# A convolution in blocks of four rows by two columns, with its filters transformed over two halves of an attention

## The chip, the cores and the metric

The program runs on one core of one Trainium2 chip. A core has a matrix engine (PE), a vector engine (DVE), an activation engine (ACT), a general engine (POOL) and a queue engine (SP). Each works through its own instructions in order and waits for the others by semaphores. The time is the device time of one launch in microseconds (us); less is better.

## The reference

Two layers, all in float32, on `x` of 4 images, 1024 channels and 32 by 32 pixels:

```python
# layer 0: attention over the 1024 pixels of an image, 16 heads of 64
q, k, v = split(x @ w_qkv.T + b_qkv)          # rotary angles and RMS norm on q and k
ctx = softmax(q @ k.T * scale) @ v
x = x + rmsnorm(ctx @ w_proj.T)
# layer 1: bottleneck, batch norm over images and pixels after each convolution
h = relu(bn(conv1x1(x, w1)))                  # 1024 -> 256 channels
h = relu(bn(conv3x3(h, w2)))                  # 256 -> 256 channels
h = bn(conv1x1(h, w3))                        # 256 -> 1024 channels
return relu(x + softplus(residual_scale) * h)
```

## The kernel before

The batch loop does one image after another: projections of q, k and v (each multiplied as blocks of a fast matrix scheme with few products), then `attention` in two halves of queries (`c` = 0 and 1) of eight head pairs each (`hp`), then the output projection. PE, POOL, DVE and ACT run in the order in which the program is written. That order is made by hand: inside `attention` the lists `late`, `ready`, `slow`, `waiting` and `extra` each give up a step at the end of a head pair, and in the projections `product_done` counts products and releases steps queued by `after`.

For one head pair PE computes the scores `sc` of eight key tiles (L790), ACT takes their exponentials into `p` (L797), DVE adds these into `den` (L814, L816), and PE multiplies `p` by `v` into `cx` (L825). `sc` has three double banks, so PE stands three tiles ahead of ACT at most. Every second head pair a product `dn` (L894) sums the denominators.

`filters` prepares the 3 by 3 filters in the second half of the last image's attention, one step for each of head pairs 1 to 7. Nine taps are loaded into three tiles (L1163); `down_sums` combines three taps in one direction (L1173 to L1176); `fours` and `twos` combine these in the other direction (L1181 to L1188); ACT scales eight results by 1/24 (L1192) and POOL queues them to memory (L1193); `ones_first` and `ones_last` make the other three sets (L1198 to L1204), with six scalings on ACT (L1205 to L1207). The filters `uw` are used in the second convolution.

The output projection follows (L491), and before its second product ACT must copy the last denominators out of a bank (L963). Then the first convolution (L1055, L1014) with partial results `h` and `c` written to memory from a ring of four tiles (`temp`).

The second convolution is done as a Winograd scheme with different block lengths in the two directions: a block of two rows by four columns of outputs comes from a window of four rows by six columns, and each of the 24 positions of the window is one matrix product over the channels. Images go in two pairs (`p`), window positions in three groups of two along the long direction (`g`, with `al` inside) and four along the short one (`j`), output channels in two halves (`f`), input channels in two (`i`). DVE makes the window transforms: `first_cols` (L1524, L1527) and `other_cols` (L1532 to L1537) along the columns, with every fourth pixel read as one operand, and `down` along the rows into the tiles `V` (L1550). `fill` (L1509) applies the norm of the first convolution on ACT. `products` (L1590) makes the products of one key `k` = (p, g, f, al) in a single PSUM bank of eight: first the half with `which` = 0, which ACT copies with swapped sides (`keep`, L1639, L1640), then the other half, which DVE adds (`take`, L1646). `outputs` (L1662 to L1675) makes the four columns from these, again with every fourth pixel written as one operand. `keep`'s copies `m` lie, for the first pair's last group and the whole second pair, in a ring of three (`big_temp`). The statistics of the second norm come from DVE for two images (L1681) and from ACT for two (`act_statistics`, L1689, L1690, whose unused output goes into `temp`). `norm2` (L1697, L1699, L1701) applies the norm. The third convolution (L1829) starts with its first input half and needs `norm2(1)` for the second.

The order in which these steps are issued is a written list at the end; `run` issues products and copies for a stretch of the keys `ks`.

Of the kernel before, what the change touches and what calls it, by code (L numbers as in the profile page):

```python
# [85 lines left out]
def program(ctx, tc, x, wblk, w2, w3, vecs, cos, sin, out, bad):  # L86
# [70 lines left out]
    wd2 = dram.tile([4, len(OUTER), len(SUMS), P, CH], F32, name=f"wd2{u}")  # L157
    u34d = dram.tile([2, 4, P, CH], F32, name=f"u34d{u}")
# [5 lines left out]
    with tc.tile_pool(name=f"st{u}", bufs=2) as st, ExitStack() as s:  # L164
# [987 lines left out]
        uw = {}  # L1152

        def filters():
# [3 lines left out]
            taps = w2.rearrange("p (c k f) -> p c k f", c=NPT, k=9)  # L1158

            def load():  # L1160
                for dx in range(3):
                    for dy, slot in enumerate((0, 1, 3)):
                        nc.gpsimd.dma_start(  # L1163
                            raw[dx][:, slot, :].rearrange("p (c f) -> p c f", c=NPT), taps[:, :, 3 * dy + dx, :]
                        )

# [3 lines left out]
            def down_sums(dx):  # L1170

                g0, g1, new, g2 = (raw[dx][:, i] for i in range(4))
                nc.vector.tensor_tensor(new, g0, g2, ALU.add)  # L1173
                nc.scalar.mul(g1, g1, 0.5)
                nc.vector.scalar_tensor_tensor(g1, new, 0.5, g1, ALU.mult, ALU.add)
                nc.vector.tensor_tensor(new, new, g1, ALU.subtract)  # L1176

            def fours():
                for j in range(4):
                    t = flat(chunk(f"u3_{j}"))  # L1180
                    nc.vector.scalar_tensor_tensor(t, raw[2][:, j], 4.0, raw[0][:, j], ALU.mult, ALU.add)  # L1181
                    plus.append(t)

            def twos():
                for j in range(4):
                    t = flat(chunk(f"u4_{j}"))
                    nc.vector.scalar_tensor_tensor(t, raw[1][:, j], -2.0, plus[j], ALU.mult, ALU.add)
                    nc.vector.scalar_tensor_tensor(plus[j], raw[1][:, j], 2.0, plus[j], ALU.mult, ALU.add)  # L1188
                    minus.append(t)
                for i, ts_ in enumerate((plus, minus)):  # L1190
                    for j, t in enumerate(ts_):
                        nc.scalar.mul(t, t, 1.0 / 24.0)  # L1192
                        nc.gpsimd.dma_start(u34d[i, j], t)  # L1193

            def ones_first():
                for h in range(2):
                    js = slice(2 * h, 2 * h + 2)
                    nc.vector.tensor_tensor(two[h], raw[0][:, js], raw[2][:, js], ALU.add)  # L1198
                    nc.vector.tensor_tensor(raw[1][:, js], two[h], raw[1][:, js], ALU.subtract)

            def ones_last():
                for h in range(2):
                    js = slice(2 * h, 2 * h + 2)
                    nc.vector.scalar_tensor_tensor(two[h], two[h], 2.0, raw[1][:, js], ALU.mult, ALU.subtract)  # L1204
                    nc.scalar.mul(raw[0][:, js], raw[0][:, js], 0.25)  # L1205
                    nc.scalar.mul(raw[1][:, js], raw[1][:, js], -1.0 / 6.0)
                    nc.scalar.mul(two[h], two[h], -1.0 / 6.0)  # L1207

            steps.append(load)
            steps.append(lambda: down_sums(0))  # L1210
            steps.append(lambda: down_sums(2))
            steps.append(lambda: (down_sums(1), fours()))
            steps.append(twos)
            steps.append(ones_first)
            steps.append(ones_last)
# [75 lines left out]
        for b in range(B):  # L1291
# [78 lines left out]
            for c in range(NCH):  # L1370
                if (b, c) == (B - 1, NCH - 1):
                    extra = filters()
# [61 lines left out]
        conv1_first(1, back[1], w)  # L1434
        for i in range(0, NH, 2):
            t_sums(back[1], None, t2[i], i, range(3, 4))
# [20 lines left out]
        if bad is not None:  # L1457
            dt = temp("dens")
            nc.sync.dma_start(dt, dens)
# [22 lines left out]
        TR, TC = H // 2, W // 4  # L1482
# [10 lines left out]
        cols = vp.tile([P, NPT, 6, 2, H + 2, TC], F32, tag="cols", name="cols")  # L1493
        pads = [vp.tile([P, H, W + 4], F32, name=f"pad{i}") for i in range(2)]
        v_tile(0, 0)
        steps_of = vp.tile([P, 4, H, TC], F32, name="steps")
        for i in range(2):
            nc.gpsimd.memset(pads[i], 0.0)
        for i in range(NPT):
            nc.gpsimd.memset(cols[:, i, :, :, :: H + 1, :].rearrange("p a b r c -> p (a b) r c"), 0.0)  # L1500
# [6 lines left out]
        def fill(p, s_, i):  # L1507
            b = PAIRS[p][s_]
            nc.scalar.activation(  # L1509
                pads[s_][:, :, 1 : W + 1], h1[b, i].rearrange("p (a c) -> p a c", a=H), AF.Relu,  # L1510
# [3 lines left out]
        def columns(t):  # L1514
            return t.rearrange("p r (c q) -> p q r c", q=4)

        def first_cols(i, which=range(2)):

            efs = {}
            for s_ in which:  # L1520
                ef = efs[s_] = temp(f"ef_{s_}_{i}").rearrange("p (x r c) -> p x r c", x=2, r=H)
                for x in range(2):
                    d, ahead_ = (columns(pads[s_][:, :, at : at + W])[:, x] for at in (1, 3))
                    nc.vector.scalar_tensor_tensor(ef[:, x], d, -4.0, ahead_, ALU.mult, ALU.add)  # L1524
            for s_ in which:
                for a, op in enumerate((ALU.add, ALU.subtract)):
                    nc.vector.tensor_tensor(cols[:, i, a, s_, 1 : H + 1, :], efs[s_][:, 1], efs[s_][:, 0], op)  # L1527

        def other_cols(s_, i):

            pad, d = pads[s_], steps_of
            nc.vector.tensor_tensor(d, columns(pad[:, :, 2 : W + 2]), columns(pad[:, :, :W]), ALU.subtract)  # L1532
            for a, by in ((2, 2.0), (3, -2.0)):
                nc.vector.scalar_tensor_tensor(
                    cols[:, i, a, s_, 1 : H + 1, :], d[:, 1], by, d[:, 2], ALU.mult, ALU.add
                )
            nc.vector.scalar_tensor_tensor(  # L1537
                cols[:, i, 4:6, s_, 1 : H + 1, :], d[:, 0:2], -4.0, d[:, 2:4], ALU.mult, ALU.add
            )

        def down(p, i, g, js=range(4)):

            c = cols[:, i, 2 * g : 2 * g + 2].rearrange("p a b (r q) c -> p q (a b) r c", q=2)
            d0, d1, d2, d3 = (c[:, k % 2, :, k // 2 : k // 2 + TR] for k in range(4))
            for j in js:
# [3 lines left out]
                out_ = v_tile(p, g)[:, i, j].rearrange("p a b (r c) -> p (a b) r c", r=TR)  # L1549
# [6 lines left out]
        first_cols(0)  # L1556
        down(0, 0, 0, (1, 2))
# [4 lines left out]
        other_cols(0, 0)  # L1562
        conv1(B - 1, 1, 0, w, yt[B - 1])
        other_cols(1, 0)
        down(0, 0, 1, (1, 2))
        conv1(B - 1, 1, 1, w, yt[B - 1], lambda: norm1(1))
        down(0, 0, 0, (0, 3))
        down(0, 0, 1, (0, 3))
        rest()
        open_pools.close()  # L1570
        ps = s.enter_context(tc.tile_pool(name=f"ps2{u}", bufs=8, space=PSUM, reuse_waits="tile"))
# [12 lines left out]
        def products(k, which, i):  # L1584

            p, g, f, al = k
            if k not in banks:
                banks[k] = ps.tile([P, CH], F32, tag="mm", name="c2_" + "_".join(map(str, k)))
            for side, j in enumerate((1, 2) if which == 0 else (0, 3)):
                nc.tensor.matmul(  # L1590
                    banks[k][:, side * QT : (side + 1) * QT],
                    uw[GROUPS[g][al], j][:, i * PL + f * P : i * PL + (f + 1) * P],
                    v_tile(p, g)[:, i, j, al].rearrange("p b t -> p (b t)"),
                    start=which == 0 and i == 0 and side == 0, stop=which == 1 and i == NPT - 1 and side == 1,
                    skip_group_check=True,
                )
# [6 lines left out]
        def x1_home(f):  # L1603

            if f % 3 not in homes:
                tags = (("V1",), ("T0", "T1"), ("T2", "cos", "sin"))[f % 3]
                homes[f % 3] = []
                for tag in tags:
                    pool, rows = (vp, B) if tag == "V1" else (tp, 2 if tag[0] == "T" else 1)
                    t = pool.tile([P, rows, N], F32, tag=tag, name=f"x1_{f}_{tag}")  # L1610
                    homes[f % 3] += [t[:, i] for i in range(rows)]
# [6 lines left out]

        order = {
# [3 lines left out]
        ks = [(p, g, f, al) for p in range(2) for g, f in order[p] for al in range(2)]  # L1623
        flat2 = lambda t: t.rearrange("p b n -> p (b n)")
        mine2 = {f: flat2(h2_all[:, f * B + 2 : f * B + 4, :]) for f in range(NPT)}

        def keep(k):

            p, g, f, al = k
            if p == 0 and g < 2:  # L1630
                m = mine2[f][:, (2 * g + al) * CH : (2 * g + al + 1) * CH]
            else:
                if al == 0:
                    mt[p, g, f] = big_temp(f"m_{p}_{g}_{f}")
                m = mt[p, g, f][:, half[al]]
            mt[k] = m
            rows = m.rearrange("p (r q c) -> p q r c", q=2, c=TC)
            x, y = (banks[k][:, i * QT : (i + 1) * QT].rearrange("p (r c) -> p r c", c=TC) for i in range(2))
            nc.scalar.mul(rows[:, 0], y, -1.0)  # L1639
            nc.scalar.copy(rows[:, 1], x)  # L1640

        def take(p, g, f):
            for al in range(2):
                m = mt[p, g, f, al].rearrange("p (r q c) -> p r q c", q=2, c=TC)
# [285 lines left out]
```

## Time and profile before

| what | us |
|---|---|
| median of three runs | 2693.37 |
| lowest and highest | 2690.72, 2693.93 |
| the profiled execution | 2693.58 |
| its span in the profile | 2691.7 |
| PE busy in it | 2611.6 |
| DVE busy | 2152.3 |
| ACT busy | 1151.5 |
| POOL busy | 462.7 |

Stages of the span, from the timeline and the busy times by stretch:

| stretch (us) | what | PE busy | DVE busy | granted PE clock |
|---|---|---|---|---|
| 0 to 1996 | images 0 to 2, projections of image 3 | 1990.69 | 1609.38 | 1.00 |
| 1996 to 2135 | last attention, first half and a little more | 139.00 | 110.62 | 1.00 |
| 2135 to 2243 | rest of the last attention | 91.40 | 87.99 | 0.94 |
| 2243 to 2328 | last output projection | 84.53 | 70.94 | 0.97 |
| 2328 to 2434 | first convolution | 102.73 | 71.87 | 0.98 |
| 2434 to 2560 | second convolution | 91.09 | 100.02 | 0.89 |
| 2573 to 2692 | third convolution, and the end | 104.28 | 89.07 | 0.94 |

A group line gives the source line, the engine, the operation and the tile names, then the busy time, the mean of one instruction and the idle time ahead of the group with what released it. In a timeline line the first number is the start, the second the length, and the bracket at the end gives the idle time ahead of it. The list of waits adds up idle time by who waited for whom: total, times, longest.

### The profile page before, as it was taken

To read this page: it belongs to the slowest core of one execution; us is meant where nothing else is said; L and a number is where in the kernel's file an instruction comes from. 1 tells how busy PE (TensorE), PEld (TensorE's weight loads), DVE (VectorE), ACT (ScalarE), POOL (GpSimd) and SP (SyncE) were. 2 spreads that over 40 slices of the span, in tenths; PEclk is the share of its full clock that TensorE was granted. 3 is DMA by queue.
4 is the path that set the end of the run, shared out by engine and by line. 5 is a ranking of instruction groups with operands and counts; after the bars stand their busy time and mean duration, and the time that the engine had idled before them with its cause. 6 is when DMAs were issued, how large, how long until landed. Compare 5 with 4: busy or idle time off the path is not lost. (4 is left out here: it accounts for less than half of the span.)

```text
span 2691.7 us, 40390 instructions
## 1 busy us (share of the span) xinstructions
PE 2611.6 (97%) x15308; PEld 1613.5 (60%) x15308; DVE 2152.3 (80%) x2601; ACT 1151.5 (43%) x1678; POOL 462.7 (17%) x610
## 2 busy tenths in 40 slices
PE   9999999999999999999999999999999989998697
PEld 4448433588887333788884335888863326746543
DVE  5668899988888877987978768888887788768787
ACT  2222566533343565233425554333445554212366
POOL 2442323101011222000111221001112320020000
PEclk9999999999999999999999999999999999999899
DMA  7887788667676442665774443666654524671166
GB/s 283 294 243 214 232 260 267 207 202 252 174 196 176 94 86 61 196 197 178 196 203 103 96 81 110 193 223 180 191 142 76 114 89 149 235 231 58 49 224 244
DMA packets 253659, 471.00 MB, mean 175 GB/s; under 512 B 32016, under 2 KB 124992, under 8 KB 253328
## 3 DMA queue, kind: packets, MB, share of 16 engines
q1 hardware_dynamic: 195008, 286.75, 33.6%
q0 software_dynamic: 50384, 164.79, 24.9%
q10 hardware_dynamic: 8064, 16.78, 1.8%
q8 instruction: 124, 2.03, 0.3%
q14 instruction: 79, 0.65, 0.1%
HBM read 331.62 MB, written 99.11 MB: 160 GB/s over the span
## 5 line engine op out<-in xcount | busy, mean ns | idle before, releaser
L797 ACT ACTIVATE p<-sc 128x1024 f32<-128x1024 f32 x512 | 479.9, 1048 | 17.1 <-PE sc L790 16.8
L790 PE MATMUL sc<-q,k 64*64 64x512 f32 x4096 | 456.7, 592 | 11.2 <-ACT p L797 11.2
L825 PE MATMUL cx<-p,to 64*64 64x512 f32 x3072 | 338.2, 589 | 0.0
L790 PEld LDWEIGHTS sc<-q,k 64*64 64x64 f32 x4096 | 150.5, 132 | 305.1 <-ACT p L797 157.3
L816 DVE TENSOR_TENSOR den<-den,p 128x1024 f32<-128x1024 f32 x192 | 237.9, 1239 | 22.9 <-ACT p L797 3.5
L816 DVE TENSOR_TENSOR den_T<-den_T,p 128x1024 f32<-128x1024 f32 x192 | 236.3, 1231 | 20.4 <-DVE den_T L816 1.4
L825 PEld LDWEIGHTS cx<-p,to 64*64 64x64 f32 x3072 | 117.2, 133 | 212.4 <-issue 211.3
L491 PE MATMUL p_y<-q,w_y 128*128 128x256 f32 x928 | 212.6, 382 | 6.7 <-issue 6.7
L486 PE MATMUL p_v<-w_v,x 128*128 128x256 f32 x928 | 210.3, 379 | 2.4 <-DVE x L457 2.3
L491 PEld LDWEIGHTS p_y<-q,w_y 128*128 128x128 f32 x928 | 176.7, 191 | 36.9 <-issue 12.1
L486 PEld LDWEIGHTS p_v<-w_v,x 128*128 128x128 f32 x928 | 176.0, 190 | 28.0 <-DVE x L457 3.3
L831 ACT COPY q<-cx 128x512 f32<-128x512 f32 x64 | 37.5, 585 | 341.3 <-PE cx L825 341.3
L491 PE MATMUL p_q<-to,w_q 128*128 128x256 f32 x672 | 152.2, 379 | 0.0
L491 PE MATMUL p_k<-to,w_k 128*128 128x256 f32 x672 | 152.2, 379 | 0.0
L491 PEld LDWEIGHTS p_q<-to,w_q 128*128 128x128 f32 x672 | 127.4, 190 | 18.4 <-issue 1.2
L491 PEld LDWEIGHTS p_k<-to,w_k 128*128 128x128 f32 x672 | 127.4, 190 | 18.4 <-issue 1.2
L771 POOL TENSOR_SCALAR q<-q,vec 128x512 f32<-128x512 f32 x42 | 81.2, 1943 | 222.1 <-DVE q L770 222.1
L1829 PE MATMUL c<-h,w3t 128*128 128x512 f32 x256 | 111.7, 599 | 5.1 <-ACT h L1699 5.1
L825 PE MATMUL cx<-p,rq 64*64 64x512 f32 x1024 | 112.7, 589 | 0.0
L486 PE MATMUL p_v<-w_v,t 128*128 128x256 f32 x384 | 90.1, 379 | 0.0
L491 PE MATMUL p_y<-to,w_y 128*128 128x256 f32 x384 | 90.1, 379 | 0.0
L1829 PEld LDWEIGHTS c<-h,w3t 128*128 128x128 f32 x256 | 49.2, 192 | 67.1 <-issue 55.7
(545 smaller groups left out, 4334.5 us busy)
## 6 DMA issues: line engine op xcount, KB each, us to landing
w_v<-wd2f SPq DMA_DIRECT2D x112, 256.0 KB
w_y<-wd2f SPq DMA_DIRECT2D x112, 256.0 KB
w_q<-wd2f SPq DMA_DIRECT2D x84, 256.0 KB
w_k<-wd2f SPq DMA_DIRECT2D x84, 256.0 KB
wd2f<-w_pre POOLq DMA_DIRECT2D x68, 256.0 KB, 3.6
q<-qs POOLq DMA_DIRECT2D x64, 256.0 KB, 5.5
k<-ks POOLq DMA_DIRECT2D x64, 256.0 KB, 4.5
x1df<-y POOLq DMA_DIRECT2D x32, 512.0 KB, 5.3
```

Source lines behind the costliest of these rows:

```text
L486: nc.tensor.matmul(o[:, q].rearrange("p (g f) -> p g f", g=2), r[:, i, q * P : (q + 1) * P], wt[:, :, i, :], skip_group_check=True, **at,)
L491: nc.tensor.matmul(o[:, q], wt[:, q, i, :], r[:, i, :], skip_group_check=True, **at)
L771: engine.tensor_scalar(cx, cx, col("bv", hp), None, ALU.add)
L790: nc.tensor.matmul(sc[keys, j], k_all[d, hp, t * P + keys.start : t * P + keys.stop], q_all[d, hp, at], start=True, stop=bad is not None,)
L797: nc.scalar.activation(p, sc, AF.Exp)
L816: nc.vector.tensor_tensor(d_, d_, p, ALU.add)
L825: nc.tensor.matmul(o[j * HD : (j + 1) * HD, i], v[keys, t, h0 : h0 + HD], probs[t][keys, j], start=(t == 0), stop=(t == N // P - 1),)
L831: nc.scalar.copy(cx, o[:, 0])
L1829: nc.tensor.matmul(os[i], w3t[k][f // NH][:, f % NH, :], h2[b, k][:, half[c]], start=(k == 0), stop=(k == NPT - 1),)
```

## The change

The block of the second convolution is turned: four rows by two columns. `first_rows` and `other_rows` now make the sums of six along the rows, where the operands are whole rows of 32 pixels, and `across` makes the four along the columns, where its operands are every second pixel of a row. In `outputs` the four rows written are whole rows, and what belongs to the columns (`pixels`, and the last two sums) is written or read at every second pixel. One bank pair of four now holds both `al` of a key, so a key has 16 products, `keep` two ACT instructions of twice the length and `take` one DVE instruction. `run` finishes the key before (`follow`) after each new one's first half. The copies `m` of the second pair get rooms of their own (`m_room`): the ring, the two tiles `hx` of the images, and the memory of `rows`. The order at the end is rewritten; `act_statistics` is cut in pieces and writes its unused output into `steps_of`; the second norm's last application is ACT's alone.

The filters' sums along the columns now come first (`filter_sums`), in the first half of the last attention, through `gd` in memory; the second half reads them back as three loads and does the rest, with the scalings by 1/24 in two steps of four (`put`). The six scalings of the other sets (`scale`) move behind the first products of the first convolution (`later_scales`). The tile `dens` for a check of the denominators is loaded by POOL's queue into a tile of another ring.

```diff
+    gd = dram.tile([3, 4, P, CH], F32, name=f"gd{u}")
-        uw = {}
+        uw, later_scales = {}, []
+        def filter_sums():
+            steps = []
+            taps = w2.rearrange("p (c k f) -> p c k f", c=NPT, k=9)
+            g = {}
+            def load(dy):
+                g[dy] = [flat(chunk(f"w2_{dy}_{i}")) for i in range(4)]
+                for dx, slot in enumerate((0, 1, 3)):
+                    nc.gpsimd.dma_start(
+                        g[dy][slot].rearrange("p (c f) -> p c f", c=NPT), taps[:, :, 3 * dy + dx, :]
+                    )
+            def halve_middle(dy):
+                nc.scalar.mul(g[dy][1], g[dy][1], 0.5)
+            def across_sums(dy):
+                g0, g1, new, g2 = g[dy]
+                nc.vector.tensor_tensor(new, g0, g2, ALU.add)
+                nc.vector.scalar_tensor_tensor(g1, new, 0.5, g1, ALU.mult, ALU.add)
+                nc.vector.tensor_tensor(new, new, g1, ALU.subtract)
+                for j in range(4):
+                    nc.gpsimd.dma_start(gd[dy, j], g[dy][j])
+            steps.append(lambda: (load(0), load(2)))
+            steps.append(lambda: halve_middle(0))
+            steps.append(lambda: (across_sums(0), halve_middle(2)))
+            steps.append(lambda: (across_sums(2), load(1)))
+            steps.append(lambda: halve_middle(1))
+            steps.append(lambda: across_sums(1))
+            return steps
...
+            def load():
+                for dy in (0, 2, 1):
+                    nc.gpsimd.dma_start(raw[dy], gd[dy].rearrange("j p f -> p j f"))
...
-            steps.append(lambda: down_sums(0))
-            steps.append(lambda: down_sums(2))
-            steps.append(lambda: (down_sums(1), fours()))
-            steps.append(twos)
-            steps.append(ones_first)
-            steps.append(ones_last)
+            steps.append(lambda: fours(range(4)))
+            steps.append(lambda: twos((0, 1)))
+            steps.append(lambda: (put((0, 1)), twos((2, 3))))
+            steps.append(lambda: (put((2, 3)), ones_first(0)))
+            steps.append(lambda: ones_first(1))
+            steps.append(lambda: (ones_last(0), ones_last(1)))
+            later_scales.extend([lambda: scale(0), lambda: scale(1)])
...
-                if (b, c) == (B - 1, NCH - 1):
-                    extra = filters()
+                if b == B - 1:
+                    extra = filters() if c == NCH - 1 else filter_sums()
...
         conv1_first(1, back[1], w)
+        for step in later_scales:
+            step()
...
-            nc.vector.tensor_tensor(d, columns(pad[:, :, 2 : W + 2]), columns(pad[:, :, :W]), ALU.subtract)
-            for a, by in ((2, 2.0), (3, -2.0)):
+            nc.vector.tensor_tensor(
+                d.rearrange("p t q w -> p (t q) w"), pad[:, 2 : H + 2, :], pad[:, :H, :], ALU.subtract
+            )
+            for a, p_, by, q_ in ((2, 1, 2.0, 2), (3, 1, -2.0, 2), (4, 0, -4.0, 2), (5, 1, -4.0, 3)):
...
-        def down(p, i, g, js=range(4)):
-            c = cols[:, i, 2 * g : 2 * g + 2].rearrange("p a b (r q) c -> p q (a b) r c", q=2)
-            d0, d1, d2, d3 = (c[:, k % 2, :, k // 2 : k // 2 + TR] for k in range(4))
+        def across(p, i, g, js=range(4)):
+            c = rows[:, i, 2 * g : 2 * g + 2].rearrange("p a b t (c q) -> p q (a b t) c", q=2)
+            d0, d1, d2, d3 = (c[:, k % 2, :, k // 2 : k // 2 + TC] for k in range(4))
...
+        def m_room(p, g, f):
+            if p == 0:
+                if g < 2:
+                    return flat2(h2_all[:, f * B + 2 : f * B + 4, :])[:, g * N : (g + 1) * N]
+                return big_temp(f"m_{p}_{g}_{f}")
+            at = order[1].index((g, f))
+            if at == 0:
+                return big_temp(f"m_{p}_{g}_{f}")
+            if at < 3:
+                return hx.tile([P, N], F32, tag="hx", name=f"m_{p}_{g}_{f}")
+            return rows[:, :, :, :, :, :].rearrange("p i a b t w -> p (i a b t w)")[:, (at - 3) * N : (at - 2) * N]
         def keep(k):
...
+            m = mt[k] = m_room(*k).rearrange("p (l q n) -> p l q n", l=2, q=2)
+            nc.scalar.mul(m[:, :, 0], banks[k][:, :, QT:], -1.0)
+            nc.scalar.copy(m[:, :, 1], banks[k][:, :, :QT])
         def take(p, g, f):
...
+            m = mt[p, g, f].rearrange("p l q n -> p (l q n)")
+            nc.vector.tensor_tensor(m, banks[p, g, f].rearrange("p l n -> p (l n)"), m, ALU.add)
...
-                rest_ = temp(f"rest_{f}_{i}")[:, :QT]
+                rest_ = steps_of[:, : QT // (4 * W)].rearrange("p t q w -> p (t q w)")
...
+        run(7, 9)
+        take(1, 0, 0)
+        take(1, 1, 0)
+        for f in range(NPT):
+            for g in range(3):
+                outputs(0, g, f)
+        run(9, 10)
+        act_statistics(0, range(4))
+        run(10, 11)
+        act_statistics(0, range(4, 8))
+        act_statistics(1, range(2))
+        take(1, 2, 0)
+        for g in range(3):
+            outputs(1, g, 0)
+        statistics(0)
+        run(11, 12)
+        act_statistics(1, range(2, 8))
+        norm2(0)
+        take(1, 0, 1)
+        outputs(1, 0, 1)
+        take(1, 1, 1)
+        outputs(1, 1, 1)
+        follow()
```

## The prediction

> **What bounds the kernel now.** I read the page's slices first. PE is the bound nearly everywhere, and only the last quarter shows holes:
>
> ```profile
> PE   9999999999999999999999999999999989998697
> DVE  5668899988888877987978768888887788768787
> PEclk9999999999999999999999999999999999999899
> ```
>
> Each digit is a fortieth (67 us). Digits 33 and 37 to 39 of PE are the places to explain; DVE is high beside them. The list of waits says who ends them:
>
> ```profile
> PE c L1590 <- ACT m L1640: 25.3, 3, 19.4
> PE sc L790 <- ACT p L797: 11.2, 1, 11.2
> PE p_y L491 <- issue: 6.7, 3, 5.8
> PE c L1829 <- ACT h L1699: 5.1, 1, 5.1
> PE c L1590 <- ACT h L1640: 5.0, 1, 5.0
> PE c L1590 <- DVE V L1550: 4.6, 2, 3.2
> ```
>
> All touch the change: 40 us in the second convolution and at its end, 11.2 once in the last attention, 5.8 once behind it. ACT is named, but ACT is 43% busy, so I read its timeline at both attention places:
>
> ```profile
> 2198.85 0.63 ACT L1192 ACTIVATE u<-u 128x512 f32<-128x512 f32 x1 [4.89 <-DVE u L1188]
> 2203.57 2.71 ACT L1192 ACTIVATE u<-u 128x512 f32<-128x512 f32 x5 [0.70 <-DVE u L1188]
> 2242.81 0.56 ACT L963 COPY rec<-dn 128x512 f32<-128x512 f32 x1
> ```
>
> and PE beside it (start, length, what, and the idle time ahead with its releaser):
>
> ```profile
> 2207.24 6.86 PE L790 MATMUL sc<-q,k 64*64 64x512 f32 x48 [11.22 <-ACT p L797]
> 2213.93 7.04 PE L825 MATMUL cx<-p,to 64*64 64x512 f32 x64
> 2243.47 3.75 PE L491 MATMUL p_y<-q,w_y 128*128 128x256 f32 x8 [5.85 <-issue]
> ```
>
> First, ACT stands before its exponentials waiting for `twos` on DVE, whose scalings come first in its order. Second, the projection's second product starts at 2243.47, just as ACT's copy L963 ends (2243.37); that copy stood behind the six scalings L1205 to L1207. "Issue" here is a bank not yet copied out.
>
> In the second convolution the chain of waits runs mostly over DVE. Two of its groups by shape (busy, mean ns, idle ahead), an operand of every fourth float and one of runs of eight:
>
> ```profile
> L1532 DVE TENSOR_TENSOR steps<-pad 128x1024 f32<-128x1024 f32 x8 | 16.3, 2036 | 0.1
> L1550 DVE TENSOR_TENSOR V<-cols 128x512 f32<-128x512 f32 x48 | 29.6, 684 | 0.1
> ```
>
> By the stretch query, from 2434.7 to 2571.7 DVE is busy 111.1 us and idle 25.9. The 19.4 comes from `big_temp`: the copy of key (1,1,0) needs the ring's room that `outputs(0, 2, 0)` reads, at the end of 15 us of DVE work.
>
> **Attention and projection.** The sixth pair's `sc` starts at 2193.13, its `cx` at 2213.93. An undisturbed pair with the same `dn` takes 8.02 from one to the other (2164.48, 2172.50), so 12.8 us are lost; the slow first products after the gap are in it. The projection's third product starts at 2247.02; from the first at 2235.63 and two of 1.73 it would be 2239.1: 7.9 lost. Together 20.7.
>
> After the change the `twos` are a head pair ahead of their scalings, so ACT waits for nothing, but `put` stays ahead of the exponentials twice, four scalings at 0.54 (2.71 for five) = 2.16. ACT idles 0.27 there, PE has three banks of lead, and ACT's pace of 0.93 a tile is slower than PE's 0.86: nearly all of the 1.9 left is paid, 1.7 the first time, 0.9 the second, where `dn` gives ACT room. 20.7 - 2.6 = 18.1. DVE fits: 9.2 a pair for `den`, at most 2.9 means, 3.4 of `twos` (0.61 and 1.06, the latter the row beside POOL's L771), 0.6 context, against 13.73; a pair beyond that borrows from the next.
>
> In the first half, `across_sums` is 0.61 + 0.69 + 0.69 = 2.0 on DVE in pairs 3, 4, 6, where DVE idles 1.4, 3.8 and 2 to 4 us. `halve_middle` adds a wait: ACT's 0.63 waits for three taps, and the next pair's eight exponentials, and with them PE, are queued behind. Issued about 2029 and 2068, wanted at 2038.2 and 2079.4: 9 and 11 us. The nearest row, L1163, lands in 3.3 at least and 12.9 in the median, behind 1.5 MB of residual; the first has no residual ahead, the second one of 512 KB (7.3 to 8.5 to land) and 1 MB of `gd`. So 0 to 6 us; I take 0.7. POOL issues 12 writes, three loads more; behind these stand the `den_T` additions, which have heads to spare. The reload of T2 waits for `dn` as L1163 does now (7.9 us), with nothing urgent behind; it lands by about 2143, wanted at 2149.
>
> A stall that goes shows what is late next: the reciprocal L964 (3.35). `ones_last` (two L1204, 2.4) still stands ahead of it on DVE. In image 2 the last sums from it end at 1676.87, with L290 and two adds, and the product reading them starts at 1677.59: 0.7 spare. Here it comes 2.8 later against the third product: 2.1 lost. The moved scalings (six at 0.95 = 5.7) meet an ACT gap of 5.2 in the first convolution (to 2339.08): 0.4 lost; w/o that gap all 5.7. Net 18.1 - 0.7 - 2.1 - 0.4 = 14.9.
>
> **Second convolution.** DVE's work, start to start: six `steps` from 2.04 to 1.14 (L290 is a plain 128x1024): -5.3. Three `ef` calls, four at 0.55 against two at 0.605: -3.0. Four sums of 256 instead of two and one of 512: +0.5. `outputs`, four times: two whole-row writes 0.90 to 0.61, two half-strided 0.90 to 0.66: -4.3. `take` 24 x 0.605 against 12 x 1.2: nothing. `across`: 44 in the stretch, unchanged in size at 0.605, if reading every second float costs nothing. DVE 111.1 - 12.1 = 99.0.
>
> That price is unknown: no row has a step of two floats. Bounds: 0.605 (runs of eight, L1550) and 1.02 (step of four, half of L1532). I take 0.605 to 0.66, since a step of four misses three floats of four and costs 1.8 cycles an element, not four; a step of two should lie at half that, or nothing. Below 0.605 nothing points.
>
> [...]
>
> Then I laid the new order out with these prices, engine by engine. PE waits 2.5 (for V of the second input half) and 3.2 (for the first copies), then not at all until the keys end at 2523; no copy waits for a room. DVE waits only for two `take`s (1.2, 2.4), for ACT's square root behind the last statistics (2.5), and about 1.4 at start and end: 7.5. Gone are 9.0 (`rest` tiles of `temp`), 5.8 (square root), 8 at takes behind the late PE. End: 2434.7 + 99.0 + 7.5 = 2541.2 for `norm2(1)`, against 2571.7. Laying out the order of before this way ends 6.5 short of the trace; 4.9 of it are products at half rate after the gaps of 5.03 (3.2) and 19.43 (1.7). I add 3. PE then starts 1.2 later (a whole `Relu`; 0.9 now): 2545.4 against 2572.57, gain 27.2. The stage becomes DVE's: 99 of 107. The third convolution's 119 us stay.
>
> [...] The row of 3.20 (2445.07) went on at full rate. [...]
>
> **Sum.** 2693.58 (profiled) - 14.9 - 27.2 = 2651.5. The median is 0.2 lower: 2651.
>
> **Rivals.** A, the half-strided operand costs like a step of four: 72 operations at about 1.06. Laid out so, `norm2(1)` ends some 24 later: 2675. For: both L1532 and L1674 pay. Against: the 1.8 cycles above. 10%.
>
> B, slower than before: the same place, but priced beyond any row. At 1.06 the stage gains about 3, so 18 in all; from 1.06 + 18/72 = 1.31 us an operation it turns. At 1.45 the sum is 2693 + 72 x 0.14 = 2703. Against it: no DVE row of this size reaches 1.2. 4%.
>
> C, ACT waits for taps: both landings at 12.9 after the last issue, some 6 and 3 us, in place of the wait removed. 2651 + 8 = 2659. For: the 12.9. Against: the traffic ahead was different. 12%.
>
> My forecast: 74%. That the stalls stay where they are, the change not doing what it says, would be 2693 less the DVE savings; the rooms and orders are plain, so it gets no share of its own.
>
> **Range.** Below: without the 3, the 2.1 and the 0.7 it is 2645, and 2 for shares I priced high: 2643. Above: C is 2659, a step of two at 0.85 is 12 more, 2663, with 3 for the clock and 2 for landings 2668. A and B lie out, 14%. A measurement here tells 0.2% (5 us) from nothing: faster 94%, same 2%, slower 4%.
>
> **What would show it.** The waits of `sc` on `p` fall to below 3 each; the third `p_y` product follows its `dn` by 4.5; L963 right behind `dn`. In the second convolution no wait over 5 on `m`, DVE about 99 busy of 107, `V` at 0.68 a record (0.605 pitch): 1.0 there proves A. ACT idle on a DMA ahead of the halvings proves C. I am wrong if `norm2(1)` follows the first `V` product by over 125 us, or a new wait stands where the removed ones were.

## The result: 2700.7 us, slower than before, and the profile after

| | us |
|---|---|
| before, median of 17 runs | 2693.07 |
| after, median of 17 runs | 2700.71 (2695.03 to 2707.4) |
| ratio, with its 95% interval | 1.0028 (1.0021 to 1.0036) |
| the profiled execution after | 2703.25 |
| its span | 2701.5 |

The forecast was 2651. The two gains that it counted came about within 1 us of their sizes, and a loss of 54 us came on top, in the one stage that it left as it was. The slices of the page show this at once:

```profile
PE   9999999999999999999999999999999999999776
DVE  5668899988888777987988778888798788859555
PEclk9999999999999999999999999999999999999898
```

The holes in slices 33 and 37 are closed. The last three, nearly all third convolution now, read 776. The list of waits on PE names them (in all us, times, longest):

```profile
PE c L1864 <- ACT h L1875: 34.2, 32, 1.9
PE c L1864 <- ACT h L1736: 9.1, 2, 5.4
PE c L1621 <- ACT h L1675: 3.5, 1, 3.5
...
PE sc L791 <- ACT p L798: 2.1, 2, 1.1
PE c L1621 <- DVE V L1580: 1.9, 1, 1.9
```

The last four lines are what is left of the waits that the prediction showed: the waits of 19.4 on `m` and of 11.2 on `p` are gone; the one on the second norm (L1736) has grown from 5.1 to 9.1. The first line has no counterpart before: 32 short waits of the third convolution's products on ACT's copies. The stretch query over that stage, from the first product of the second input half to the end, gives its price (start and end, length, then busy time and instructions of PE, PEld, DVE, ACT and POOL, granted clock, DMA share, GB/s). First before, then after:

```profile
2572.60:2691.70 119.10, 104.68 (x240) 46.08 (x240) 89.47 (x132) 84.33 (x119) 0.00 (x0) 0.94 0.65 230
```
```profile
2527.90:2701.50 173.60, 124.85 (x240) 47.10 (x240) 87.87 (x125) 87.27 (x119) 0.00 (x0) 0.88 0.45 158
```

(The profile has two records for each product that the program issues; "products" are such records from here on.) The same 240 products take 54.5 us more: 34.3 of it PE stands idle, 20.2 it is longer busy. Between the marks ahead of it the change did what it should. From the first `sc` of image 3 to the first `V` product: 438.7 before (1996.02 to 2434.70), 423.1 after (1993.62 to 2416.70), 15.6 less. From there to the second input half of the third convolution: 137.9 and 111.2, 26.7 less. So -15.6 - 26.7 - 2.4 (the earlier images in this execution) + 54.5 = +9.8, the difference of the two spans.

PE's timeline shows the form of the loss, here four of the trains of eight products:

```profile
2557.49 3.70 PE L1864 MATMUL c<-h,w3t 128*128 128x512 f32 x8 [0.78 <-ACT h L1875]
2561.97 3.70 PE L1864 MATMUL c<-h,w3t 128*128 128x512 f32 x8 [0.78 <-ACT h L1875]
2567.58 5.40 PE L1864 MATMUL c<-h,w3t 128*128 128x512 f32 x8 [1.91 <-ACT h L1875]
2573.80 3.70 PE L1864 MATMUL c<-h,w3t 128*128 128x512 f32 x8 [0.83 <-ACT h L1875]
```

And ACT's beside it:

```profile
2563.99 0.69 ACT L1875 ACTIVATE h<-c,vec 128x512 f32<-128x512 f32 x1 [2.08 <-PE c L1864]
2565.84 0.29 ACT L1146 ACTIVATE sc<-mv,eps_bn 128x1 f32<-128x1 f32 x1 [1.17 <-DVE mv L1144]
2566.57 0.39 ACT L1150 ACTIVATE sh<-sc,bea,mv 128x1 f32<-128x1 f32 x1 [0.43 <-DVE sc L1148]
2566.86 0.67 ACT L1875 ACTIVATE h<-c,vec 128x512 f32<-128x512 f32 x1
```

A train is the second bank of one image's tile and the first bank of the next one's. After it PE stops until ACT has ended its copy out of that first bank (2566.86 + 0.67, PE goes on at 2567.58). Mostly this is one copy, 0.78; once in a block of output channels the copy stands behind the norm of the block before, 1.91.

The lines of the change that do it are few. The account of the change above leaves them out, and the prediction gave them no term. The third convolution's results had a single-bank tile each; with the pool's tiles now of two banks, both halves of an image share one:

```diff
-            os = [ps.tile([P, CH], F32, tag="mm", name=f"c3_{f}_{i}") for i in range(B * NCH)]
+            os = [
+                o for i in range(B) for o in [ps.tile([P, NCH, CH], F32, tag="mm", name=f"c3_{f}_{i}")]
+            ]
+            os = [os[i // NCH][:, i % NCH] for i in range(B * NCH)]
```

My theory T: reads and writes of a tile are ordered as a whole, so that a product into the second bank must wait for a read of the first, which it does not touch. Its rivals: R, four large rooms come free too late; D, what lies before the stage leaves ACT, DVE or the loads behind.

### The profile page after: what moved, and what is told of

It reads as the page before. It is cut to its first block, busy times and chain, and to the rows that moved or that the text cites. A ratio compares the mean times of both kernels' runs of the same rounds, so it can differ in the third digit from the quotient of the medians.

```text
span 2701.5 us, 40389 instructions
## 1 busy us (share of the span) xinstructions
PE 2625.6 (97%) x15308; PEld 1613.3 (60%) x15308; DVE 2132.5 (79%) x2581; ACT 1153.0 (43%) x1654; POOL 473.5 (18%) x626
## 4 chain that ended last, share of the span: by engine, by line
PE 60%; ACT 4%; DVE 3%; DMA 1%; issue 1%; POOL 0%; ACTq 0%; DVEq 0%
PE cx L826 11%; PE sc L791 11%; PE p_y L492 9%; PE p_v L487 8%; PE p_q L492 6%; PE p_k L492 6%; PE c L1864 3%; PE c L1621 2%; ACT h L1875 1%; PE c L1056 1%; PE c L1015 1%; ACT h L1847 1%; DVE den L817 1%; DMA h1df<-c 1%; PE c1s L1056 1%
## 5 line engine op out<-in xcount | busy, mean ns | idle before, releaser
L798 ACT ACTIVATE p<-sc 128x1024 f32<-128x1024 f32 x512 | 479.8, 1049 | 15.6 <-PE sc L791 15.3
L487 PEld LDWEIGHTS p_v<-w_v,x 128*128 128x128 f32 x928 | 176.4, 190 | 26.7 <-DVE x L458 1.4
L1864 PE MATMUL c<-h,w3t 128*128 128x512 f32 x256 | 135.1, 675 | 43.3 <-ACT h L1875 34.2
L1877 DVE BATCH_NORM_STATS2 s<-h 128x6 f32<-128x512 f32 x63 | 43.6, 693 | 75.2 <-ACT h L1875 75.2
```

The source lines that it names most:

```text
L487: nc.tensor.matmul(o[:, q].rearrange("p (g f) -> p g f", g=2), r[:, i, q * P : (q + 1) * P], wt[:, :, i, :], skip_group_check=True, **at,)
L798: nc.scalar.activation(p, sc, AF.Exp)
L1864: nc.tensor.matmul(os[i], w3t[k][f // NH][:, f % NH, :], h2[b, k][:, half[c]], start=(k == 0), stop=(k == NPT - 1),)
L1877: nc.vector.bn_stats(stats[:, i, :], h)
```

## Experiments on the loss

**Order alone.** The tiles stay; the products of both banks are issued ahead of the two copies:

```diff
+            def pair(b, ks):
+                for c in range(NCH):
+                    for k in ks:
+                        nc.tensor.matmul(
+                            os[b * NCH + c], w3t[k][f // NH][:, f % NH, :], h2[b, k][:, half[c]],
+                            start=(k == 0), stop=(k == NPT - 1),
+                        )
...
-            for i, k in order:
+            for i in range(B * NCH):
                 b, c = divmod(i, NCH)
-                nc.tensor.matmul(
-                    os[i], w3t[k][f // NH][:, f % NH, :], h2[b, k][:, half[c]],
-                    start=(k == 0), stop=(k == NPT - 1),
-                )
-                if k < NPT - 1:
-                    continue
+                if c == 0:
+                    pair(b, (1,) if f == 0 else range(NPT))
```

> The changed kernel with one thing reordered: in the third convolution the products of both banks of a tile are issued before ACT's two copies out of it; the same tiles, products and copies. Theory T (a product into the second bank of a two-bank tile waits until ACT has read the first bank of that tile, because reads and writes of a tile are ordered as a whole): the 32 waits of 0.8 to 1.9 us go, with the half-rate products behind them; from the first product of the third convolution's second input half to the end 119 to 122 us instead of 173.6, so 2647 us (2643 to 2655). Rival R (four tiles of two banks are released too late, one whole tile at a time, so that PE runs out of rooms): the release comes no earlier in this order, 2695 to 2705 us. Rival D (what comes before the third convolution leaves ACT, DVE or the loads of x1 behind, and PE waits for them): 2695 to 2705 us.

Measured 2650.84 (ratio to before 0.984, 0.9825 to 0.9855). All 32 waits are gone; PE's timeline has the rest of the stage as one unbroken line:

```profile
2527.43 105.40 PE L1862 MATMUL c<-h,w3t 128*128 128x512 f32 x240 [4.53 <-ACT h L1736]
```

The rooms and everything ahead are as they were, so R and D fall. I call this one the reordered kernel.

**Single banks.** The order stays; `ps` is closed after the second convolution and a pool of eight `[P, CH]` tiles takes its place:

```diff
...
+        conv2_banks.close()
+        ps = s.enter_context(tc.tile_pool(name=f"ps3{u}", bufs=8, space=PSUM, reuse_waits="tile"))
...
-                o for i in range(B) for o in [ps.tile([P, NCH, CH], F32, tag="mm", name=f"c3_{f}_{i}")]
...
+            os = [ps.tile([P, CH], F32, tag="mm", name=f"c3_{f}_{i}") for i in range(B * NCH)]
```

> The changed kernel with the third convolution's results in eight tiles of one bank, as in the kernel before, from a pool of their own; the order of products and copies is that of the changed kernel. T and R: 2647 us (2643 to 2655), within 3 us of the run with the pairs reordered if T is the whole of it; by R that run stays near 2700 and this one alone falls. D: 2695 to 2705 us.

Measured 2649.74 (0.9839, 0.9824 to 0.9854). The old order runs without a stop once the banks are tiles of their own:

```profile
2518.91 111.84 PE L1864 MATMUL c<-h,w3t 128*128 128x512 f32 x256 [12.78 <-issue]
```

The one wait ahead of it, 12.78, I put down to the new pool, which opens only when the old one is closed; in the reordered kernel two waits, 5.42 and 4.53, stand in its place. So PE can write a bank while ACT reads another, here for 111.84 us without a stop; the wait lay in how the program names them.

**The tile in the kernel before.** The reverse, only this put into the kernel before, whose second convolution keeps its eight banks:

```diff
...
+        conv2_banks.close()
+        ps = s.enter_context(tc.tile_pool(name=f"ps3{u}", bufs=4, space=PSUM, reuse_waits="tile"))
...
-            os = [ps.tile([P, CH], F32, tag="mm", name=f"c3_{f}_{i}") for i in range(B * NCH)]
+            os = [
+                o for i in range(B) for o in [ps.tile([P, NCH, CH], F32, tag="mm", name=f"c3_{f}_{i}")]
+            ]
+            os = [os[i // NCH][:, i % NCH] for i in range(B * NCH)]
```

> The kernel before with only the third convolution's results put into four tiles of two banks, from a pool of their own, order unchanged. T: the same 32 waits as in the changed kernel appear, +45 to +57 us on 2693, so 2738 to 2750 us. R: the same. D: nothing, 2690 to 2697 us.

Measured 2742.46, +48.6 (1.0186, 1.0169 to 1.0204), and the list of waits on PE has a new head:

```profile
PE c L1835 <- ACT h L1846: 33.3, 32, 2.0
```

Its loss is 6 smaller than the 54; part of that is that its trains of four in the first block run at 1.98, where two of the changed kernel take 3.78. T is shown from both sides: taken away two ways, and made alone.

**The longer gaps.** Only 34 of the 54 us are waits. The two-bank tile and both orders stay as in the changed kernel; the norm of a block is issued behind the next block's first copy:

```diff
                 if not last:
                     nc.vector.bn_stats(stats[:, i, :], h)
+                if f > 0 and i == 0:
+                    norms[f - 1] = negative_norm(prev, f - 1)
...
-            sc, sh = norms[f] = negative_norm(stats, f)
+            prev = stats
+        sc, sh = norms[NT - 1] = negative_norm(prev, NT - 1)
```

> The changed kernel with its two-bank tiles and its order of products and copies; only the norm of each output block of the third convolution is issued behind the next block's first copy instead of ahead of it. The waits of 1.91 us are those where the copy out of a first bank stands behind this norm on ACT; six of the eight profiled ones were followed by products at half rate for 1.7 us more. Theory (the tile-wide wait costs one copy, 0.78 us, each; the 1.91 and the half rate behind it come from ACT's order and the longer gap): all 32 waits are 0.78 to 0.83, no half-rate groups within the blocks, 8 x 1.13 = 9 and some 5 x 1.7 = 8.5 less, 2683 us (2679 to 2688). Rival (any run of gaps every 4 us brings the half rate, whatever their length): the groups of 5.40 stay, 2690 to 2693 us.

Measured 2686.29 (0.997, 0.9959 to 0.9981). The waits come to 26.6 instead of 34.2, and no train of eight takes over 3.70. Of the waits of 1.9 one is left, 1.89 near the start of the stage, ahead of the first norm; I had expected none:

```profile
2585.59 3.70 PE L1864 MATMUL c<-h,w3t 128*128 128x512 f32 x8 [0.83 <-ACT h L1875]
2590.11 3.70 PE L1864 MATMUL c<-h,w3t 128*128 128x512 f32 x8 [0.83 <-ACT h L1875]
```

The first is the place of the former 1.91 in its block. (In its profile the earlier images run 4.6 us later; the stage itself takes 155.7, 17.9 less.) So the 20.2 of longer busy time splits, by my estimate: five trains at 5.40 (8.5), two of four products at 3.78 instead of 1.98 (3.6) and the slow first two (1) are half rate, about 13. The rest, 7, is that a train which runs empty takes 3.70 where eight in a row take 3.49 (104.68 for 240 in the kernel before).

## Experiments on the parts that were forecast

The runs below were timed in three sets, in which the kernel before measured 2693.83, 2692.86 and 2692.84; the reordered kernel is of the first set, and all that stand against it below are of the other two. Differences of 1 us between sets mean nothing.

**The filters alone**, on the kernel before: `filter_sums`, `put` in two steps and `later_scales` as in the diff, with the taps' indices exchanged so that the second convolution stays as it was:

```diff
-                            raw[dx][:, slot, :].rearrange("p (c f) -> p c f", c=NPT), taps[:, :, 3 * dy + dx, :]
+                        g[dy][slot].rearrange("p (c f) -> p c f", c=NPT), taps[:, :, 3 * dx + dy, :]
```

> The kernel before with the filters' part of the change alone (sums over both halves of the last attention, put in two steps, six scalings moved to the first convolution); second and third convolution as before. By the trace of the changed kernel the second convolution starts 15.6 us earlier after the drift of the earlier images is taken off, and nothing behind it depends on that: 2693 - 15.6 = 2677.5 us (2673 to 2682). Rival: some of it is cover for DMA or the clock and is given back in the first or second convolution: 2684 us or more.

Measured 2678.19 (0.9939, 0.9925 to 0.9952): 15.6 less than before's 2693.83. The term of 14.9 stands.

**The block alone**: the reordered kernel with the filters' code of before, the indices exchanged:

```diff
-                if b == B - 1:
-                    extra = filters() if c == NCH - 1 else filter_sums()
+                if (b, c) == (B - 1, NCH - 1):
+                    extra = filters()
```

> The kernel with the reordered products of the third convolution (2650.8 us), with the filters prepared as in the kernel before: all in the second half of the last attention, nothing in its first half, scalings in two steps. Theory (the two parts are independent): the 15.6 us that the filters alone gave come back, 2666.5 us (2663 to 2671). Rival (the parts share a gain, since a later start of the second convolution is covered by its DVE work): 2658 us or less.

Measured 2666.35 (0.9903, 0.9888 to 0.9919), 15.5 above 2650.84. The two parts add, to the 1 us of the sets.

**Scalings back**, in the reordered kernel:

```diff
-            steps.append(lambda: (ones_last(0), ones_last(1)))
-            later_scales.extend([lambda: scale(0), lambda: scale(1)])
+            steps.append(lambda: (ones_last(0), ones_last(1), scale(0), scale(1)))
```

> The kernel with the reordered products (2650.8 us), but the six scalings of the other three filter sets stand in the last step of the filters again, in the last head pair. Theory: ACT's copy of the denominators stands behind them and the projection's second product waits for it as before, 5 us and its half-rate products: +5 to +8, 2656 to 2659 us. Rival (with the put a head pair earlier ACT has caught up by then): 2650 to 2653 us.

Measured 2660.24, +9.4, more than I expected, though by the theory's mechanism. ACT stands 4.4 us for `ones_last` on DVE, then does the scalings, and only then the copy of the denominators:

```profile
2232.61 1.06 ACT L1230 ACTIVATE t_w<-t_w 128x1024 f32<-128x1024 f32 x1 [4.40 <-DVE u_cos L1225]
...
2237.36 0.56 ACT L964 COPY rec<-dn 128x512 f32<-128x512 f32 x1
```

PE's second product starts at 2238.02, after 7.36 us of idling; it was 5.85 before.

**Put at once**, in the reordered kernel:

```diff
-            steps.append(lambda: twos((0, 1)))
-            steps.append(lambda: (put((0, 1)), twos((2, 3))))
-            steps.append(lambda: (put((2, 3)), ones_first(0)))
+            steps.append(lambda: (twos(range(4)), put(range(4))))
+            steps.append(lambda: ones_first(0))
             steps.append(lambda: ones_first(1))
-            steps.append(lambda: (ones_last(0), ones_last(1)))
+            steps.append(lambda: ones_last(0))
+            steps.append(lambda: ones_last(1))
```

> The kernel with the reordered products (2650.8 us), but the four sums of twos and their eight scalings stand in one step of one head pair, as in the kernel before; the filter sums over the first half and the later scalings stay. Theory (what took the 11.2 us wait away is that the scalings lie a head pair behind their sums): ACT waits for twos on DVE before its exponentials, PE shows one wait of 9 to 11 us on p, +8 to +12, 2659 to 2663 us. Rival (the shorter work of the half alone is enough, DVE has caught up): +0 to +3, 2651 to 2654 us.

Measured 2653.19 (0.9857, 0.9842 to 0.9872, against 0.9825 to 0.9855 with the steps apart). My range of 2659 to 2663 was missed, and the time lies in the rival's (2651 to 2654). By time this can hardly be told from nothing, but the wait is back, earlier in the half:

```profile
PE sc L791 <- ACT p L798: 7.1, 1, 7.1
```

From the first `sc` to the first `V` product it takes 426.4 instead of 421.1 in the reordered kernel, 5.2 more; the changed kernel, whose program is the same there, took 423.1, so some 2 of it can be chance. `p_y` starts 7.0 later by the same count and then runs without the 1.7 of waits that it has there; that this is because the filters' sums behind `put`, all but one, come a head pair sooner was not tried by itself. So splitting `put` is worth 3 to 5 in these profiles, half of what I expected or less, and the single wait was 4 shorter than the one of before, whose half also held the first sums. The medians alone leave it open.

**Rooms**, in the reordered kernel; the outputs move because the ring can't turn otherwise:

```diff
         def m_room(p, g, f):
...
-            at = order[1].index((g, f))
-            if at == 0:
-                return big_temp(f"m_{p}_{g}_{f}")
...
+            return big_temp(f"m_{p}_{g}_{f}")
...
+        for f in range(NPT):
+            for g in range(3):
+                outputs(0, g, f)
         run(7, 9)
         take(1, 0, 0)
         take(1, 1, 0)
-        for f in range(NPT):
-            for g in range(3):
-                outputs(0, g, f)
```

> The kernel with the reordered products (2650.8 us), but all copies m of the second pair lie in the ring of three again, and the first pair's outputs stand ahead of the takes of (1, 0, 0) and (1, 1, 0), without which the ring can't turn. Theory (the rooms are what took the 19.4 us wait away): ACT's copy of (1, 1, 0) waits for the outputs that read (0, 2, 0), some 17 us later than now; PE shows a wait of 10 to 19 us on m in the second convolution and its last keys end some 15 us later; +8 to +20, 2659 to 2671 us, most likely 2665. Rival (the turned block left enough DVE time free, the rooms are not needed): 2649 to 2654 us.

Measured 2662.75, +11.9 (0.9886, 0.9871 to 0.9901). The wait on `m` is back, and DVE then waits 10.0 at the norm:

```profile
PE c L1621 <- ACT m L1670: 10.4, 3, 7.2
```

The kernel differs in the rooms and in the order that they force; the two are not told apart.

**A further order, and the best version.** In the changed kernel DVE stands idle for ACT's square root of `norm2(0)`, which lies behind six pieces of statistics:

```profile
2511.93 0.16 DVE L1130 RECIPROCAL sc<-sc 128x1 f32<-128x1 f32 x1 [4.25 <-ACT sc L1129]
```

In the reordered kernel (4.26 there):

```diff
-        act_statistics(1, range(2, 8))
         norm2(0)
+        act_statistics(1, range(2, 8))
```

> The kernel with the reordered products (2650.8 us), with one order changed: norm2(0) is issued ahead of ACT's last six statistics of the second output half. In the trace DVE stands 4.26 us idle for norm2(0)'s square root, which lies behind 6.5 us of these on ACT, and everything up to norm2(1) is later by that. Theory (DVE's chain sets the start of the third convolution): 4 us less, 2646.8 us (2645 to 2649). Rival (ACT's statistics are then late for norm2(1), which waits for them instead): 2650 to 2653 us.

Measured 2647.94 (0.9836, 0.9823 to 0.985), 2.9 less. The two intervals overlap, so the time alone does not show the gain; the profile does. From the first `V` product to the second input half it takes 105.8 instead of 109.5 us; ACT's statistics are done 1.4 before `norm2(1)` asks for them. The same two lines exchanged in the kernel with single banks:

> The changed kernel with eight single banks in the third convolution and with norm2(0) ahead of ACT's last six statistics. Theory: the two gains add as far as norm2(1) goes, whose first application ends at 2524 us as in the run with the norm first; from there 104.9 us of products and a tail of 14.8, 2646 us (2644 to 2648), the fastest of all. Rival (the first products, which wait in this kernel until the second convolution's last bank is read, are then the later end): 2648 to 2650 us.

Measured 2644.89, 0.9821 of before (0.9808 to 0.9834), the lowest median of all, 48 us under the kernel before. Its interval overlaps with those of the single banks and of the norm first.

## Why the prediction was wrong, step by step

- **The step that failed** is one sentence: "The third convolution's 119 us stay." It took 173.6. I read the change of the banks' pool as belonging to the second convolution, laid that one's order out engine by engine, and carried the third over from the trace of before, though its tiles were new. All rivals were about DVE, ACT and DMA in the stages that I had costed, so the range of 2643 to 2668 held no case of this kind, and its other side (B, 4%) was a mechanism that did not occur; that B's 2703 lies near the 2700.7 is chance.
- **The price could have been worked out**, had I known that the two banks of a tile are ordered as one. The copy of 512, L1840, was in the trace of before at a mean of 0.68, and 32 tiles with one such stop each are 22 at least.
- **Attention and projection**: 14.9 forecast, 15.6 by the marks and 15.6 alone. Of its terms, `put` stalls PE by 1.12 + 0.99 (2.6 taken) and the halvings by 0.62 (0.7 taken; ACT waited 1.69 for the third load). The reciprocal was sized too large: PE waits 0.66 for it, 2.1 was taken. Moving the scalings was worth more than the 5.8 they hid, by the run with them back; there ACT first waits 4.40 for DVE's sums, where it waited 1.74 in the kernel before.
- **Second convolution**: 27.2 forecast, 26.7 by the marks. DVE's busy time is 97.3 (99.0). Its idle time is larger, 13.6 against 7.5 and the 3 of drift: the square root costs 4.25 (2.5 taken) and a `take` 2.62 (2.4). The terms' errors cancel, so the nearness of the sum is luck in part. The 3 for the clock in the range is shown by no run; in the changed kernel the 16 products behind the gap of 3.45 us took 5.24, start to start, and the next 16 took 3.45, so 1.8 were lost there, and 0.3 on the eight behind the gap of 1.93 (2.01 against 1.73).
- **Rival C** happened in kind, an ACT wait of 1.69 for a tap, and cost 0.6 and not 8.
- **The sum without the failed step.** The forecast of 2651 is what the reordered kernel takes, 2650.8. That they agree so closely is luck too: in its profile the two stretches are shorter by 17.5 and 28.3, not 14.9 and 27.2, and the third convolution takes 2.6 longer than before.
- **Two misreadings.** The last low digit of PE before is the 40th, not the 39th. And the row of 3.20 (2445.07) did not go on at full rate. Its second pair and the four after it are slow, 1.13 and 1.91 where 0.59 and 1.03 are usual, some 1.4 us lost:

```profile
2445.07 0.70 PE L1590 MATMUL c<-V,u_cos 128*128 128x256 f32 x2 [3.20 <-DVE V L1550]
2445.68 1.13 PE L1590 MATMUL c<-V,u_sin 128*128 128x256 f32 x2
2446.60 1.91 PE L1590 MATMUL c<-V,t_w 128*128 128x256 f32 x4
```

- **Rivals A and B.** A step of two floats costs nothing, in these two groups by form of after (busy, mean ns):

```profile
L1580 DVE TENSOR_TENSOR V<-rows 128x512 f32<-128x512 f32 x48 | 29.6, 684 | 0.1
...
L1712 DVE TENSOR_TENSOR h<-m,sd 128x512 f32<-128x512 f32 x6 | 3.9, 684 | 0.0
```

It is 684 ns, as `V` took with runs of eight, so A and B fall. Reading alone (L1580, 684) and writing and reading together (L1712, 684) show it alike. The 1.8 of the prediction equals the ratio of 2.04 to 1.14, a row with a step of four against a plain one of its size; the profile counts no cycles, and no run here shows why a step of four pays and one of two does not.

## What to carry to other kernels

When a change alters the shape of a pool's tiles, list every user of that pool and lay each out anew, also those that the change is not about. In these kernels a tile of two banks made one piece of what were two (32 waits, 34.2 us): if one engine fills its second half while another drains the first, either issue all writes of the tile ahead of its reads or keep a tile for each bank. (The pools of the second and third convolution here were opened with `reuse_waits="tile"`; another setting was not tried.) Short waits that repeat can cost more than their sum where PE is the bound: here 34 us of waits cost 54.

## What the runs showed of the hardware

- PE's rate can fall after gaps shorter than the 2.5 and 3.2 of the prediction. In the changed kernel five of seven gaps of 1.9 us between trains of eight were followed by a train of 5.40 instead of 3.70. The kernel before with two-bank tiles has five of seven too. Of the trains of eight after gaps of 0.78 to 0.83, 20 in each of these two runs and 27 in the one with the norm issued later, none took over 3.70. Why two of seven went on at 3.70 is not shown.
- The length of the gap alone does not decide. In the kernel before, two gaps of 2.68 and 3.21 in the second convolution were followed by eight products at full rate (1.99), though one of 1.37 (to 2496.07) was followed by eight that took 2.41. Nor does unbroken work ahead of the gap: 19 and 7 us of it lay ahead of the first two, 41 ahead of the third. What decides stays open.

```profile
2543.01 1.99 PE L1590 MATMUL c<-V,t_w 128*128 128x256 f32 x8 [2.68 <-ACT m L1640]
...
2553.39 1.99 PE L1590 MATMUL c<-V,u 128*128 128x256 f32 x8 [3.21 <-ACT m L1640]
```

- The half rate can come late. After the gap of 3.45 us in the second convolution (to 2433.52) the first products ran at full rate for 1.0 us and then at half for about 3, much as behind the 3.20 above:

```profile
2434.05 0.60 PE L1621 MATMUL c<-V,u_sin 128*128 128x256 f32 x2
2434.49 1.50 PE L1621 MATMUL c<-V,t_w 128*128 128x256 f32 x4
2435.78 1.06 PE L1621 MATMUL c<-V,u_cos 128*128 128x256 f32 x2
```

- The spread of the changed kernel's runs, 12.4 us, is three times that of before, 4.2 (both 17 runs); a train more or less at half rate is 1.7 us, which would make such a spread. That was not tested by itself.
